# A state-space filter and a gated low-rank feed-forward on one core: first group in a fixed order, two weight sums by transfers, token halves as heads

## The chip, the core and the metric

The kernel runs on one NeuronCore of a Trainium2 chip. The metric is the device time of one execution in microseconds (us). Before the change it is 1004.41 us, the median of three runs (1003.79 to 1004.69).

The core has TensorE (PE: matrix products from SBUF into PSUM), VectorE (DVE), ScalarE (ACT), GpSimd (POOL) and SyncE (SP, which here only issues transfers). ACT and POOL issue transfers as well. All transfers move over 16 DMA engines.

## What is computed

Each of 64 channels h is filtered along 1024 positions with a kernel that comes from 64 complex exponentials, is masked by length, and the 1024-vector of each of 64 x 64 tokens then goes through a gated mixture of 64 low-rank experts:

```python
def cond(u, length, log_dt, C, log_A_real, A_imag, D):     # u: 64 x 64 x 1024
    mask = (jnp.arange(Lq) < length[:, None]).astype(u.dtype)
    u_m = u * mask[:, None, :]
    # K[h, l] = 2 Re sum_n Cs[h, n] exp(dtA[h, n] * l)
    kernel = _get_kernel(log_dt, C, log_A_real, A_imag, Lq)
    y = irfft(rfft(u_m, 2 * Lq) * rfft(kernel, 2 * Lq))[..., :Lq]
    y = y + u_m * D[:, None]
    return y * mask[:, None, :]

def ffn(x, A, B, Wr):                                       # 64 experts of rank 16
    scores = xf @ Wr.T
    top_vals, top_idx = jax.lax.top_k(scores, 16)
    G = zeros(N, 64); G[top_idx] = softmax(top_vals)
    h = jnp.einsum('nd,krd->nkr', xf, A)
    return jnp.einsum('nkr,kdr->nd', h * G[:, :, None], B) * 2.0

out = x + ffn(cond(x, ...), A, B, Wr)
```

A and B are seen as 1024 x 1024 matrices (64 experts times rank 16). All arithmetic is in float32.

## The kernel before

**Groups.** The 64 channels are cut into eight groups of eight (`HG`), so a group has 8 x 64 = 512 tokens (`TOK`). The kernel has two stages: for each group the filter, the gates and the product with A; then, over all groups, the product with B. The change lies in the first stage, and nearly all of it in group 0 and in what comes before it.

**Filter of a group** (`tables`, `conv`). A position is block times 128 plus offset. `tables(g)` makes, for four pairs of channels, the powers `w` of the exponentials (ScalarE: exp, sin, square; VectorE: phases), from them `b`, and by two products with the identity (`pb`, L277 and L279) the matrix `bt` that turns a block into a state. A column of `bt` plus D gives `kc`. Its transpose `pk` (L292) goes by a small transfer to `krows` in DRAM, and is read back as `toep`, a Toeplitz matrix for each channel (L295, L297). `turn` holds the step over one block. `tables` is a generator, and its callers advance it step by step.

`conv(g)` takes pairs of channels. `into_states(i)` (L555, L560) makes the state that each block adds, four products per pair, evicted by ScalarE. `recur` (L563 to L573) carries states over the seven blocks on VectorE: 18 small instructions per pair, two pairs interleaved in group 0. `out_of(i)` multiplies x with `toep` (L581) and the states with `w` (L587) into `pc`, and VectorE masks `pc` into `y` (L593).

**Product with A** (`first`, `seven`). It is a Strassen-Winograd product with seven multiplications instead of eight: left factors from the quarters of A, right factors from the quarters of y. A right quarter is half of the features by half of the tokens. Before, a token half is half of the batch: `y` has the shape `[P, NBLK, NS2, HG, HB]`, and each half takes 32 of 64 batch entries of all eight channels. `right_factors` (VectorE, four instructions) makes the sums. `seven` runs the products in the order 1, 6, 2, 7, 5, 4, 3 for each of two row ranges j (0 and 2); each product is eight matmuls. Products 1 and 2 accumulate in one bank, 5 and 3 in another. Product 1 reads right quarter 11, product 2 quarter 21, with the left factors a11 and a12, and neither needs a sum.

**Left factors.** `quarters` (L156) loads the quarters of A on SP's queue, eight transfers of 512 KB, and x tiles follow. `factors_by_identity` (L182) forms s1 = a21 + a22, s2 = a11 + s1 and s4 = a12 + s2 in four PSUM banks, by products with the identity, then a11 + a21 into the place of a21. ScalarE copies each bank out. Product 3 uses s4, and product 7 the new a21.

**Gates** (`gates`, `spread_gates`). Scores `psh` (L640), `psc` (L649), the top 16 by `max` and `match_replace` on VectorE, softmax; a transpose `pg` (L685), a copy, a transfer to `gt_dram`, and eight loads of 256 KB (`gx`, POOL's queue) that spread each gate over 16 rows. `finish` multiplies the products with `gx` on POOL (L719) and, for quarter 11, on VectorE (L726).

**What sets the order.** A scheduler orders the instructions of each engine ahead of time; within an engine they then run in that order. Parts are held as written: `manual_schedule(engines={V.engine})` (`first_order`, L355) fixes VectorE from the parameters to the mask (L475), and `keep_in_program_order` fixes single instructions. PSUM pools limit what may be in flight: `ps_f` has four banks (sums, products, and `pc` of odd pairs of group 0), `ps_c` two (`pc`), `ps_k` two (`pb`, `pk`, `pu`, scores).

The start is written as: parameters together with six steps of `tables(0)` (L419), the scales alpha and beta (L458), all s1, s2 and s4 sums (L463), the rest of `tables(0)` (L466), the mask (L469 to L473). Then `conv(0)` runs with the remaining sums as its steps, then `gates(0)`, `first(0)`.

Of the kernel before, what the change touches and what calls it, by code (L numbers as in the profile page):

```python
# [44 lines left out]
P = 128  # L45
# [14 lines left out]
HB = NB // NS2  # L60
# [32 lines left out]
def body(ctx: ExitStack, tc, x, xo, lens, par, dvec, at, bm, wt, cst, out):  # L93
# [62 lines left out]
    def quarters(wpool, w, name, queue):  # L156


        where = (("s3", 1, 0), ("a22", 1, 1), ("a11", 0, 0), ("a12", 0, 1))
        a = [factor(wpool, name, t) for t, m, k in where]  # L160

        def load(n, i):
            t, m, k = where[n]
            tc.keep_in_program_order(queue.dma_start(
                a[n][:, i : i + 2, :],
                w[:, k * KH + i : k * KH + i + 2, m * (L // 2) : (m + 1) * (L // 2)],
            ))

        for n, i in ((0, 0), (1, 0), (0, 2), (1, 2), (2, 0), (2, 2), (3, 0), (3, 2)):
            load(n, i)  # L170
        return a
# [10 lines left out]
    def factors_by_identity(a21, a22, a11, a12, out):  # L182
# [14 lines left out]
        for k in range(KH):  # L197
            add(banks[k], a11[:, k, :])
            nc.scalar.copy(s2[:, k, :], banks[k])
            yield  # L200
        for k in range(KH):
            add(banks[k], a12[:, k, :], last=True)
            nc.scalar.copy(s4[:, k, :], banks[k])
            yield
        for k in range(KH):
            bank = ps_c.tile([P, L // 2], F32, tag="pc", name=f"sum3_{k}")
            add(bank, a11[:, k, :], first=True)
            add(bank, a21[:, k, :], last=True)
            nc.scalar.copy(a21[:, k, :], bank)
            yield  # L210
# [4 lines left out]
    wa_quarters = quarters(wp, at, "wa", nc.sync)  # L215
# [9 lines left out]
    def tables(g):  # L225
# [37 lines left out]
        bt = tp.tile([P, GP, 2 * P + 2], F32, tag="bt", name=f"bt_{g}")  # L263
        kc = tabp.tile([P, HG], F32, tag="kc", name=f"kc_{g}")
        for i in range(GP):
# [5 lines left out]
            nc.scalar.activation(b[:, 0, :], re, AF.Copy, scale=alpha[:, j : j + 1])  # L271
            nc.scalar.activation(b[:, 1, :], re, AF.Copy, scale=nbeta[:, j : j + 1])
# [8 lines left out]
            nc.scalar.copy(bt[:, i, :], pb)  # L281
            yield
        turn = tab2.tile([P, 3, GP], F32, tag="turn", name=f"turn_{g}")
        V.tensor_copy(turn[:, 0:2], w[:, :, :, P])
        ts(turn[:, 2], turn[:, 1], -1.0, ALU.mult)
        h0 = g * HG
        tt(kc.rearrange("p (i a) -> p i a", a=2), bt[:, :, 2 * P :],
           d_sb[:, h0 : h0 + HG].rearrange("p (i a) -> p i a", a=2), ALU.add)
        yield
        row = krows[h0 : h0 + 1, :]  # L290
        pk = ps_k.tile([HG, P], F32, tag="pk", name=f"pk_{g}")
        nc.tensor.matmul(pk, lhsT=kc, rhs=ident, start=True, stop=True)  # L292
        ks = tabp.tile([HG, P], F32, tag="ks", name=f"ks_{g}")
        nc.scalar.copy(ks, pk)
        nc.sync.dma_start(krows[h0 : h0 + HG, P - 1 :], ks)  # L295
        toep = tp.tile([P, HG, P], F32, tag="toep", name=f"toep_{g}")
        nc.sync.dma_start(  # L297
            toep, bass.AP(row.tensor, row.offset, [[1, P], [KROW, HG], [1, P]]))
# [57 lines left out]
    first_order.enter_context(tc.manual_schedule(engines={V.engine}))  # L356
    log_both = par_sb[:, 0:2, :].rearrange("p a h -> p (a h)")
# [59 lines left out]

    steps0 = tables(0)
    together(some(steps0, 6), real_part(), angle())  # L419
# [41 lines left out]
    wa, wb = [], []  # L461
    marks = {}
    sums = factors_by_identity(*wa_quarters, wa)  # L463
    for _ in some(sums, 12):
        pass
    for _ in steps0:  # L466
        pass

    lens_f = prep.tile([P, NB], F32, tag="lensf", name="lens_f")  # L469
    V.tensor_copy(lens_f, lens_sb)  # L470
    mask = const.tile([P, NBLK, NB], F32, tag="mask", name="mask")
    tt(mask, feat.unsqueeze(2).to_broadcast([P, NBLK, NB]),
       lens_f.unsqueeze(1).to_broadcast([P, NBLK, NB]), ALU.is_lt)  # L473
# [681 lines left out]
```

## Time and profile before

| | |
|---|---|
| median of three runs | 1004.41 us |
| the profiled execution, whole | 1004.42 us |
| its span | 1002.6 us, 12158 instructions |
| granted TensorE clock | 0.998 |
| span up to psh of group 0 | 55.87 us |
| TensorE busy from 0 to 30, 30 to 56 us | 23.21 and 24.62 us |
| VectorE busy in the same | 18.55 and 22.64 us |
| TensorE busy from 56 to 135 us | 78.78 of 79 us |
| transfers before x6 has landed | 6.8 MB by 22 us |

The span is that of the instructions; the time of the execution has 1.8 us around it. A line of the time line gives start, length from the first to the last of its instructions, engine, source line, operation, tiles out<-in with their shapes, and the number of instructions; square brackets hold the idle time before it and what ended it. One fp32 matmul is two instructions. A line of the stages gives the window, its length, the busy time and number of instructions of PE, PEld, DVE, ACT and POOL, then granted clock, busy share of the 16 DMA engines and GB/s. Names in this profile are those of the program without their numbers: `was`, `waa` are quarters and sums of A, `h` a product with A, `s` a state (before 560 us), `ty` a right factor, `p_...` a parameter.

### The profile page before, as it was taken

To read this page: it belongs to the slowest core of one execution; us is meant where nothing else is said; L and a number is where in the kernel's file an instruction comes from. 1 tells how busy PE (TensorE), PEld (TensorE's weight loads), DVE (VectorE), ACT (ScalarE), POOL (GpSimd) and SP (SyncE) were. 2 spreads that over 40 slices of the span, in tenths; PEclk is the share of its full clock that TensorE was granted. 3 is DMA by queue.
4 is the path that set the end of the run, shared out by engine and by line. 5 is a ranking of instruction groups with operands and counts; after the bars stand their busy time and mean duration, and the time that the engine had idled before them with its cause. 6 is when DMAs were issued, how large, how long until landed. Compare 5 with 4: busy or idle time off the path is not lost.

```text
span 1002.6 us, 12158 instructions
## 1 busy us (share of the span) xinstructions
PE 985.1 (98%) x4416; PEld 738.4 (74%) x4416; DVE 717.5 (72%) x1672; ACT 165.8 (17%) x339; POOL 330.8 (33%) x278
## 2 busy tenths in 40 slices
PE   7999999999999999999999999998999999999998
PEld 3367666686676676677677578887888888888887
DVE  6887778587587587676646649778965786686674
ACT  5436041131141041031001100000000000000000
POOL 0002023122123113114103202245655673654555
PEclk9999999999999999999999999999999999999999
DMA  7113316315405315315315154473474367267432
GB/s 273 64 53 112 126 42 184 137 52 154 137 22 184 118 40 163 137 43 163 115 65 158 48 198 163 158 272 137 158 264 167 126 211 271 85 210 253 132 119 105
DMA packets 66189, 140.86 MB, mean 140 GB/s; under 512 B 9362, under 2 KB 17874, under 8 KB 66130
## 3 DMA queue, kind: packets, MB, share of 16 engines
q1 hardware_dynamic: 49376, 94.54, 27.4%
q0 software_dynamic: 15744, 44.07, 14.0%
q10 hardware_dynamic: 1010, 1.48, 0.6%
q8 instruction: 35, 0.57, 0.2%
q14 instruction: 24, 0.20, 0.1%
HBM read 92.79 MB, written 47.25 MB: 140 GB/s over the span
## 4 chain that ended last, share of the span: by engine, by line
PE 96%; DVE 3%; DMA 1%; issue 0%; SPq 0%; DVEq 0%
PE h L502 38%; PE s L933 33%; PE pc L581 6%; PE pc L587 5%; PE pu L555 5%; PE psh L640 3%; PE sum L190 2%; PE pb L277 1%; DMA waa<-in_at 1%; PE psc L649 1%; PE pb L279 1%; DVE t L788 0%; DVE y L593 0%; PE pg L685 0%; PE pk L292 0%
## 5 line engine op out<-in xcount | busy, mean ns | idle before, releaser
L318 DVE SCALAR_TENSOR_TENSOR s<-s,turn 128x64 f32<-128x64 f32 (+1 forms) x576 | 146.0, 303 | 36.7 <-ACT s L560 30.2
L502 PE MATMUL h<-y,waa 128*128 128x256 f32 x512 | 122.7, 384 | 0.0
L502 PE MATMUL h<-y,was 128*128 128x256 f32 x512 | 117.8, 381 | 0.0
L502 PE MATMUL h<-ty,was 128*128 128x256 f32 x512 | 116.4, 380 | 0.0
L502 PEld LDWEIGHTS h<-y,waa 128*128 128x128 f32 x512 | 93.7, 190 | 27.0 <-issue 15.4
L502 PEld LDWEIGHTS h<-y,was 128*128 128x128 f32 x512 | 96.1, 190 | 19.9 <-issue 7.5
L502 PEld LDWEIGHTS h<-ty,was 128*128 128x128 f32 x512 | 96.6, 190 | 16.7 <-issue 3.9
L719 POOL TENSOR_TENSOR hg<-h_p,gx 128x512 f32<-128x512 f32 x16 | 26.8, 1678 | 223.1 <-DVE h_p L318 215.4
L719 POOL TENSOR_TENSOR hg<-h_u,gx 128x512 f32<-128x512 f32 x32 | 49.5, 1546 | 136.2 <-DVE h_u L307 136.1
L593 DVE TENSOR_TENSOR y<-pc,mask 128x512 f32<-128x512 f32 x64 | 42.5, 684 | 37.0 <-PE pc L587 37.0
L947 ACT COPY p<-s 128x512 f32<-128x512 f32 x28 | 16.4, 586 | 317.4 <-PE s L933 317.4
L696 POOL DMA_DIRECT2D gx<-gt_dram x56 | 33.5, 625 | 97.2 <-DMA gt_dram<-gt 90.3
L812 POOL TENSOR_TENSOR o<-o,acc_a 128x512 f32<-128x512 f32 x32 | 48.5, 1535 | 47.8 <-ACT acc_a L830 21.7
L581 PE MATMUL pc<-x,toep 128*128 128x512 f32 x128 | 62.0, 607 | 0.0
L502 PE MATMUL h<-ty,waa 128*128 128x256 f32 x256 | 58.8, 382 | 0.0
L307 DVE TENSOR_TENSOR hg<-hg 128x512 f32<-128x512 f32 x64 | 42.8, 689 | 21.4 <-POOL hg L719 20.5
L560 ACT COPY s<-pu 128x448 f32<-128x448 f32 x64 | 33.9, 532 | 140.8 <-PE pu L555 140.4
L587 PE MATMUL pc<-s,w 64*128 64x448 f32 x256 | 56.8, 562 | 0.0
L502 PEld LDWEIGHTS h<-ty,waa 128*128 128x128 f32 x256 | 47.9, 190 | 10.7 <-issue 4.6
L555 PE MATMUL pu<-x,bt 128*64 128x448 f32 x256 | 55.5, 553 | 0.0
L812 POOL TENSOR_TENSOR o<-o,b_room 128x512 f32<-128x512 f32 x32 | 49.9, 1580 | 9.8 <-DVE b_room L307 9.8
L307 DVE TENSOR_TENSOR o<-o,s 128x512 f32<-128x512 f32 x52 | 35.4, 681 | 23.6 <-PE s L933 18.5
(225 smaller groups left out, 1627.8 us busy)
## 6 DMA issues: line engine op xcount, KB each, us to landing
x<-in_x SPq DMA_DIRECT2D x32, 512.0 KB
hg_dram<-hg POOLq DMA_DIRECT2D x16, 1024.0 KB, 6.0
o<-in_xo SPq DMA_DIRECT2D x64, 256.0 KB
out<-o SPq DMA_DIRECT2D x64, 256.0 KB
gx<-gt_dram POOLq DMA_DIRECT2D x56, 256.0 KB, 6.6
qy<-hg_dram SPq DMA_DIRECT2D x28, 512.0 KB
r<-hg_dram SPq DMA_DIRECT2D x26, 512.0 KB
hg_dram<-hg POOLq DMA_DIRECT2D x16, 768.0 KB, 4.4
```

The source lines that it names most:

```text
L307: V.tensor_tensor(out=o, in0=a, in1=b, op=o_)
L318: V.scalar_tensor_tensor(out=o, in0=a, scalar=s, in1=b, op0=o1, op1=o2)
L502: nc.tensor.matmul(bank[:, ii, :], lhsT=fac[n - 1][:, k, (j + ii) * P : (j + ii + 1) * P], rhs=rf[n - 1][:, k, :], start=(first and ii == ...
L555: nc.tensor.matmul(pu[hh * NS : (hh + 1) * NS, :], lhsT=bt[:, i, (1 - c) * P + hh * NS : (1 - c) * P + (hh + 1) * NS], rhs=xt[:, hh, : NCH ...
L560: nc.scalar.copy(s[:, c], pu.rearrange("p (k b) -> p k b", b=NB))
L581: nc.tensor.matmul(pc, lhsT=toep[:, 2 * i + hh, :], rhs=xt[:, hh, :], start=True, stop=False)
L587: nc.tensor.matmul(pcs[hh][:, NB:], lhsT=w[o : o + NS, c, i, 1:], rhs=s[o : o + NS, c].rearrange("p k b -> p (k b)"), start=False, stop=(c ...
L593: marks["y"] = V.tensor_tensor(out=y[:, :, :, 2 * i + hh, :], in0=pcs[hh].rearrange("p (k s b) -> p k s b", s=NS2, b=HB), in1=mask.rearran ...
L696: i = queue.dma_start(gx[:, ii, :], gt_dram[g, c * n : (c + 1) * n, :].unsqueeze(1).to_broadcast([n, RANK, TOK]),)
L719: G.tensor_tensor(out=o, in0=a, in1=b, op=op)
L812: tc.keep_in_program_order(G.tensor_tensor(out=o, in0=a, in1=b, op=op_))
L933: nc.tensor.matmul(bank[:, ii, :], lhsT=left_[i - 1][:, k, ii * P : (ii + 1) * P], rhs=right_[i - 1][:, k, :], start=(first and ii == 0 an ...
```

## The change

- **Loads.** The first 1 MB of A comes in four transfers of 256 KB instead of two of 512 KB (`fine`).
- **Sums.** `factors_by_identity` makes s1 and s2 only. `other_sums` adds a11 onto a21 by accumulating transfers from DRAM, loads a12 into the place of s4, and accumulates s2 onto it, six transfers of 512 KB on POOL's queue.
- **Tables of group 0.** `b` is scaled by VectorE instead of ScalarE. `kc`, `pk`, `krows` and `toep` are made for pairs 0 and 1 as soon as their `bt` is there, then for pairs 2 and 3.
- **Order.** ScalarE is held in written order too (`first_copies`), until the sums are done: one sum ahead of the parameters' sine, seven after the scales. `conv(0)` advances `tables(0)` itself, and closes VectorE's written order after the mask.
- **Token halves.** A half is now four of eight channels with all batch entries: `y` is `[P, NBLK, NS2, HH, NB]`, and the host arranges xo and out accordingly. Half 0 is thus complete once pairs 0 and 1 are.
- **Products in group 0.** `out_of` is cut into `inside` (Toeplitz part) and `across` (states). In `seven` product 2 comes second for j = 0 of group 0, and the right factors of that group are made only after it. Product 1 is issued between `inside` and `across` of pairs 2 and 3, product 2 after the `across`. A fourth state tile uses room of `y`.
- **Group 1.** Its tables are issued after the last state copy of group 0 as well as after its last mask.

```diff
-HB = NB // NS2
+HH = HG // NS2
...
+        if fine:
+            for i in range(2):
+                load(0, i, 1)
+                load(1, i, 1)
+        for n, i in ((0, 0), (1, 0), (0, 2), (1, 2), (2, 0), (2, 2), (3, 0), (3, 2))[2 * fine :]:
             load(n, i)
...
         for k in range(KH):
-            add(banks[k], a11[:, k, :])
+            add(banks[k], a11[:, k, :], last=True)
             nc.scalar.copy(s2[:, k, :], banks[k])
             yield
-        for k in range(KH):
-            add(banks[k], a12[:, k, :], last=True)
-            nc.scalar.copy(s4[:, k, :], banks[k])
-            yield
-        for k in range(KH):
-            bank = ps_c.tile([P, L // 2], F32, tag="pc", name=f"sum3_{k}")
-            add(bank, a11[:, k, :], first=True)
-            add(bank, a21[:, k, :], last=True)
-            nc.scalar.copy(a21[:, k, :], bank)
-            yield
+    def other_sums(a21, a22, a11, a12, s4, s2):
+
+        for k in range(0, KH, 2):
+            G.dma_start(a21[:, k : k + 2, :], at[:, k : k + 2, : L // 2], accum_op=ALU.add)
+        for k in range(0, KH, 2):
+            tc.keep_in_program_order(
+                G.dma_start(s4[:, k : k + 2, :], at[:, KH + k : KH + k + 2, : L // 2]))
+        for k in range(0, KH, 2):
+            G.dma_start(s4[:, k : k + 2, :], s2[:, k : k + 2, :], accum_op=ALU.add)
...
+        def rows(i, n):
+
+            w_, row = 2 * (n - i), krows[h0 + 2 * i : h0 + 2 * i + 1, :]
+            pk = ps_k.tile([w_, P], F32, tag="pk", name=f"pk_{g}_{i}")
+            nc.tensor.matmul(pk, lhsT=kc[:, 2 * i : 2 * n], rhs=ident, start=True, stop=True)
+            ks = tabp.tile([HG, P], F32, tag="ks", name=f"ks_{g}_{i}")[:w_, :]
+            nc.scalar.copy(ks, pk)
+            nc.sync.dma_start(krows[h0 + 2 * i : h0 + 2 * n, P - 1 :], ks)
+            nc.sync.dma_start(toep[:, 2 * i : 2 * n, :],
+                              bass.AP(row.tensor, row.offset, [[1, P], [KROW, w_], [1, P]]))
...
-            nc.scalar.activation(b[:, 0, :], re, AF.Copy, scale=alpha[:, j : j + 1])
-            nc.scalar.activation(b[:, 1, :], re, AF.Copy, scale=nbeta[:, j : j + 1])
+            for c, by in enumerate((alpha, nbeta)):
+                if g == 0:
+                    ts(b[:, c, :], re, by[:, j : j + 1], ALU.mult)
+                else:
+                    nc.scalar.activation(b[:, c, :], re, AF.Copy, scale=by[:, j : j + 1])
...
+            if g == 0 and i == 2:
+                kernels(0, 2)
+                rows(0, 2)
             yield
...
+    first_copies = ExitStack()
+    first_copies.enter_context(tc.manual_schedule(engines={nc.scalar.engine}))
...
     steps0 = tables(0)
-    together(some(steps0, 6), real_part(), angle())
+    next(steps0)
+    for _ in some(sums, 1):
+        pass
+    together(some(steps0, 5), real_part(), angle())
...
-    for _ in some(sums, 12):
+    for _ in some(sums, 7):
         pass
-    for _ in steps0:
-        pass
+    first_copies.close()
+    other_sums(*wa_quarters, *wa[2:6:3])
...
         yield
+        if second_early:
+            product(2, c11)
+            yield
         p6 = product(6)
...
+        if g == 0:
+            step(1)
         into_states(0)
         into_states(1)
         if g == 0:
-            step(KH)
+            step(3)
+            masks()
+            first_order.close()
+            step(1)
+            prep_ctx.close()
         recur(0, 1)
         if g == 0:
             into_states(2)
-            out_of(0)
             into_states(3)
+            first_two = inside(0), inside(1)
+            across(*first_two[0], True)
+            across(*first_two[1])
             recur(2, 3)
-            out_of(1)
-            out_of(2)
-            out_of(3)
+            last_two = inside(2), inside(3)
+            yield
+            across(*last_two[0], True)
+            across(*last_two[1])
             return
...
-    for _ in conv(0, sums, got):
+    steps = conv(0, steps0, got)
+    next(steps)
+    hp = pool(left, "hp", 1, "left")
+    y = got.pop()
+    spread = {}
+    products, done = counted(first(0, y, spread)), [0]
+    ahead(products, 1)
+    for _ in steps:
         pass
-    y = got.pop()
-    products = None
+    ahead(products, 1)
...
-                with tc.issue_after(marks["y"].ins):
+                with tc.issue_after(marks["y"].ins), tc.issue_after(marks["s"].ins):
```

## The prediction

> **What bounds the kernel.** The page first: which engine is full, and which engine the last chain runs through.
>
> ```profile
> PE 985.1 (98%) x4416; PEld 738.4 (74%) x4416; DVE 717.5 (72%) x1672; ACT 165.8 (17%) x339; POOL 330.8 (33%) x278
> PE 96%; DVE 3%; DMA 1%; issue 0%; SPq 0%; DVEq 0%
> ```
>
> TensorE is the bound: work taken off it pays, unless it then waits. The waits of TensorE say where it does (total, times, longest):
>
> ```profile
> PE sum L190 <- DMA was<-in_at: 5.5, 1, 5.5
> PE s L933 <- DVE acc_a L307: 3.2, 1, 3.2
> PE psh L640 <- DVE y L593: 1.7, 2, 1.4
> PE pg L685 <- DVE sa L307: 1.3, 1, 1.3
> ```
>
> Almost nothing after the start. The change works in the first 56 us, so I read the time line there (start, length):
>
> ```profile
> 5.54 2.05 PE L190 MATMUL sum<-was,cst_sb 128*128 128x512 f32 x2 [5.54 <-DMA was<-in_at]
> 16.03 8.75 PE L190 MATMUL sum<-waa,cst_sb 128*128 128x512 f32 x20
> 29.75 3.33 PE L555 MATMUL pu<-x,bt 128*64 128x448 f32 x16
> 55.87 3.65 PE L640 MATMUL psh<-y,wt_sb 128*64 128x512 f32 x16 [1.38 <-DVE y L593]
> 63.91 3.62 PE L502 MATMUL h<-ty,was 128*128 128x256 f32 x16
> ...
> 15.94 0.19 DVE L307 TENSOR_TENSOR p_s<-p_s 128x32 f32<-128x32 f32 x1 [1.84 <-ACT p_s L404]
> 24.39 0.35 DVE L318 SCALAR_TENSOR_TENSOR b<-w,p_nbeta,b 128x128 f32<-128x128 f32 x1 [3.34 <-ACT b L271]
> 32.09 10.71 DVE L318 SCALAR_TENSOR_TENSOR s<-s,turn 128x128 f32<-128x128 f32 x44 [1.74 <-ACT s L560]
> ```
>
> Before psh at 55.87 TensorE is never idle after 8.8, yet VectorE waits on ScalarE at 14 to 24 us, because ScalarE is evicting sums. Two chains run side by side: TensorE's work, and parameters, b, states, recurrence, masks on VectorE. Removing TensorE work leaves the second, so both have to be timed.
>
> **TensorE's account.** One weight-sum matmul (two instructions) costs 0.86 us warm (8.77 us for ten from 16.03). The sums s4 (4) and a21 (8) go: 12 x 0.86 = 10.3 us. Two products move ahead of psh; one is 3.46 us (16 instructions, 0.216 us apart), so 6.9 us is done early. One more small pk costs 0.3 us. Work before psh was 55.87 - 5.54 - 1.22 - 1.38 = 47.7 us; it becomes 44.6, of which 6.9 later work. If TensorE idled as before (8.1 us), the gain would be about 10 us. The question is the idle time.
>
> **VectorE's chain, dated step by step** from the instruction order of the changed program and the durations above:
> - The fixed ScalarE order puts one eviction, not two, ahead of the sine table. The two waits on ScalarE (1.84 and 0.24 us) go: the scales end at 20.95 - 2.1 = 18.9.
> - b of group 0 moves to VectorE: per pair two tensor_scalar at about 0.14 (between the 0.09 that a 32-wide one holds the engine and the 0.34 of a 516-wide one) and two scalar_tensor_tensor at 0.29, so 0.86. Four end at 22.3; a first pair at 19.8 feeds TensorE, where before the first was at 24.8. The 3.34 us wait goes. VectorE pays 8 x 0.14 = 1.1 us, in time it spent waiting. Kernel column, turn and mask (0.6) bring it to 23.6.
> - pu of pairs 0 and 1: 1.65 us each from 21.1, ScalarE 0.53 behind each bank: the second state is ready at 25.1. The recurrence proper starts there, not at 32.09.
> - Each half of the recurrence is 36 instructions at 0.243 (10.71/44), 8.75 us; with the few that start alone, the first ends at 33.0. In the meantime TensorE does pb, pk, pu of pairs 2 and 3 and four toep products (1.91 a pair) until 33.9, then across pairs 0 and 1 (1.71 each) until 37.3.
> - The second half, with four masks (0.60 apart) between: 33.0 to 44.2. TensorE waits for the first masks (ps_c has two banks) from 37.3 to 38.9, runs toep of pairs 2 and 3 to 42.7, waits 0.3 for y of pair 1, then product 1 (43.0 to 46.5), across (49.9), product 2 (53.3). The last mask ends at 51.3, so psh no longer waits: 53.3 instead of 55.87, **2.55 us earlier with 6.9 us of products done: 9.5 us**.
>
> **Toeplitz in two halves.** The trace has one transfer of 512 KB, issued at 31.46 and moving until 34.7, 3.2 us. The half has its kernel rows by 25.7, is issued near 27.1 and lands by about 29.6; TensorE asks at 30.1. SP has nothing else queued there: the x loads of the next group come behind, and wait for TensorE anyway. The cover is 0.5 us; each us beyond is paid.
>
> **Transfers in place of sums.** No row shows an accumulating transfer. The a21 sum and the s4 load and sum are 3.1 MB on POOL's queue, issued from about 10 us, once the s1 products have read a21. Product 7 wants them near 61, so their own time is hidden, and POOL has nothing until the gate loads at 72. What they can hurt is the x loads:
>
> ```profile
> 18.00:19.00 1.00, 1.00 (x3) 0.38 (x2) 0.76 (x4) 1.00 (x3) 0.00 (x0) 1.00 1.04 394
> 22.00:23.00 1.00, 1.00 (x4) 0.47 (x3) 0.00 (x0) 1.00 (x4) 0.00 (x0) 1.00 0.00 0
> ```
>
> The DMA share is 1.04 until 20 us: the engines are full while these transfers come in. Adding up the rows, x of pairs 0 and 1 lands at about 16.4 and 18; they are needed at 21.1 and 22.75. The Trainium skill, "DMA: Bandwidth & Descriptors", section "Issuing engines are not separate DMA queues", says that transfers of all issuers share the same engines and interleave. By it, at half of 390 GB/s, x arrives at 21.6 and 24.3: 1.5 us is paid. If the cover by the row alone held, 0. The ends are 0 and 2.7 (everything shared from 10 us on). I take **1.5**, since the row shows no free engine.
>
> **Clock.** The first sums at 5.54 took 1.19 us an instruction, later ones 0.59: the array starts cold, at half speed. The trace has one later gap of a like size, in the product with B, and the stages behind it (first figure behind the busy times: granted clock) show what it costs:
>
> ```profile
> 681.46 3.46 PE L933 MATMUL s<-b_room,ey 128*128 128x256 f32 x8 [3.23 <-DVE acc_a L307]
> ...
> 681.00:682.00 1.00, 0.55 (x2) 0.52 (x3) 1.00 (x3) 0.00 (x0) 0.00 (x0) 0.91 1.07 436
> 682.00:683.00 1.00, 1.00 (x3) 0.73 (x3) 1.00 (x3) 0.00 (x0) 0.00 (x0) 0.50 0.55 221
> ```
>
> 3.23 us of idleness, then half speed for some 3.4 us (681.9 to 685.3): 1.7 us lost. The Trainium skill, "TensorE: Matmul & The Clock Gate", Part 1, puts the bound at about 3.4 us of idleness, in windows that run freely. Both speak against this change: TensorE now idles at about 13.5 to 15.3 and 18.2 to 19.8, with 3 us of work between. By row and rule each gap is too short, 0; if a window with so little work counts as idle, pb and pu from 19.8 run at half speed for 3.4 us and the states come 1.7 us later. I take 0.
>
> **After psh.** The gates need psc, then 7.6 us of VectorE (61.46 to 69.04); TensorE has 22 matmuls of products against 20 before, 9.5 us. VectorE has w and b for the next group between, so pg waits about **0.5 us**. VectorE then meets the gating of c11, a wait for the gate load, ahead of kc, on which pk and all of TensorE behind it hang. The first two gate loads land 3.9 us after issue:
>
> ```profile
> gx<-gt_dram POOLq DMA_DIRECT2D x2, 256.0 KB, 3.9
> ```
>
> Issued at about 72, they are there at 76.3; TensorE reaches pk at 78. Hidden by 1 us. In group 1 TensorE has 21 matmuls between pu of pair 1 and pu of pair 2, as before; from group 2 on its order is the old one. The layout leaves mask, products and transfers their sizes, and the mask writes runs of 64 instead of 32. I cost that at 0: VectorE has room in the groups (52 of 75 us busy from 210 to 285), so a change of either sign in its 0.68 is covered by TensorE.
>
> **Sum.** 9.5 - 1.5 - 0.5 = 7.5 us. The profiled execution took 1004.42 with a span of 1002.6, so 1.8 us lies outside; it is the median (1004.41). Span 995.1, time **996.9 us**.
>
> **Rivals.**
> - *A slower start.* States arrive later still, by the cold array (1.7) and the later x of pair 1 (2.7 instead of 1.5); VectorE's chain hands it on whole. For it: full DMA engines, two new gaps. Against: the gaps are short. Gain 7.5 - 2.9 = 4.6: about 999.8.
> - *Given back in group 0 and 1.* The products that used to cover gates and gate loads are spent: if pg, kc and the group 1 recurrence each wait about 2.2 us (between the 1.3 of pg and the 3.2 of the longest late wait above), 6.6 go: about 1003.5. Against: 21 or 22 matmuls still lie there.
> - *Slower: accumulation starves x.* If an accumulating byte holds a DMA engine long enough, x of pair 1 is late by more than the gain. Gain ends when it lands 9 us after 22.75, at 32. From 10 us on 22 us x 390 GB/s = 8.6 MB of engine time; the loads up to that x need 3.0, leaving 5.6 for 1.05 plain and 2.1 accumulated: it decides from 2.2 times a plain byte, if served ahead of x. At 3 times (7.4 + 3.0 MB, 26.6 us from 10) x lands at 36.6, 13.9 late in all against 1.5 counted: 996.9 + 12.4 = about 1009. For it: no row prices accumulation. Against: queues interleave, and half of the accumulation waits for s2 and the s4 load.
>
> **How the numbers follow.** Forecast 63%, slow start 19%, given back 10%, starved 8%. A measurement of this kernel tells 0.2%, 2 us, from no change. The first two are faster; of the third a part lies on each side of 1002.4: faster 0.87, same 0.06, slower 0.07. The range goes from 993.8 (no contention, no pg wait, and 1 us of VectorE's chain over-counted) to 1001.8 (the slow start, and one of the waits of the next rival with it).
>
> **What would show it.** Right: no psh wait, psh near 53 to 55 with two h products before it; 24 fewer sum instructions; the first long recurrence at 25 to 27; TensorE idle before psh 8 to 12 us. x late: pu waits for in_x. Cold: pb or pu at twice 0.39 and 0.54 us an instruction. Given back: waits of pg or pk on VectorE over 2 us. The forecast is wrong if psh comes after 58, or if groups beyond 1 change length.

## The result, and the profile after

The changed kernel took 1002.38 us (median of 12 executions, 996.38 to 1005.30), beside 1004.18 us for the kernel before, measured with it. The ratio is 0.997, with a 95% interval from 0.9956 to 0.9983: faster by a little, and far from the 996.9 us of the forecast. Four more executions of the same kernel (e11 below) gave 998.68 us, so the median of all 16 is 1000.8. The two intervals for this one kernel (the other is 0.9927 to 0.9956) only touch, so that a difference of two or three us between medians proves little here without its profile. The kernel before spreads over 2 us, this one over 9. The profiled execution took 1004.54 us, with a span of 1002.8: it lies near the upper end of the range, and its loss is larger than that of the median.

The page of the changed kernel: busy time by engine, and the engines of the chain that ended last.

```profile
PE 977.8 (98%) x4394; PEld 736.2 (73%) x4394; DVE 716.7 (71%) x1681; ACT 160.1 (16%) x324; POOL 334.4 (33%) x284
PE 91%; DMA 4%; DVE 3%; issue 0%; POOL 0%; ACT 0%; SPq 0%; DVEq 0%
```

TensorE has 22 instructions and 7.3 us less to do, as the diff says (24 of sums go, two of pk come). But transfers now hold 4% of the chain instead of 1%. The waits of TensorE (total, times, longest) name them:

```profile
PE pu L601 <- DMA x<-in_x: 4.0, 2, 3.8
PE pu L601 <- ACT s L606: 2.9, 2, 2.2
PE pk L287 <- DVE kc L338: 2.4, 3, 1.5
PE pc L627 <- DMA toep<-krows: 1.5, 1, 1.5
PE psh L702 <- DVE y L644: 0.3, 1, 0.3
PE pg L747 <- DVE sa L338: 0.3, 1, 0.3
```

The waits for y and sa that the change was to shorten are nearly gone (1.7 to 0.3 us, 1.3 to 0.3). In their place stand x (4.0), toep (1.5) and two that come through ScalarE and VectorE (2.9, 2.4). The time line dates them (start, length, instructions, idle time before and what ended it):

```profile
19.79 0.49 PE L309 MATMUL pb<-cst_sb,b 128*128 128x130 f32 x2
...
21.70 1.72 PE L601 MATMUL pu<-x,bt 128*64 128x448 f32 x8 [0.24 <-DMA x<-in_x]
27.19 3.25 PE L601 MATMUL pu<-x,bt 128*64 128x448 f32 x8 [3.77 <-DMA x<-in_x]
30.37 0.80 PE L309 MATMUL pb<-cst_sb,b 128*128 128x130 f32 x2
...
39.83 3.70 PE L627 MATMUL pc<-x,toep 128*128 128x512 f32 x8 [1.54 <-DMA toep<-krows]
...
60.61 3.65 PE L702 MATMUL psh<-y,wt_sb 128*64 128x512 f32 x16
```

The first tables come at 19.79, as forecast (19.8). Then x of pair 1 is 3.8 us late, the same eight instructions take 3.25 us instead of 1.72, toep is late too, and psh starts at 60.61 instead of the forecast 53.3 (54.8 with the late x that was priced in). The windows of 1 us (busy time of PE, PEld, DVE, ACT, POOL, then granted clock, DMA share, GB/s) show what happened to the transfers and the clock:

```profile
22.00:23.00 1.00, 1.00 (x8) 0.35 (x4) 1.00 (x6) 0.30 (x1) 0.00 (x0) 1.00 1.10 257
26.00:27.00 1.00, 0.00 (x0) 0.00 (x0) 0.00 (x0) 0.00 (x0) 0.00 (x0) 0.50 1.05 418
32.00:33.00 1.00, 1.00 (x5) 0.88 (x4) 0.25 (x1) 0.27 (x2) 0.00 (x0) 0.59 0.95 172
```

At 22 us, where the DMA engines stood idle before, they are full and move only 257 GB/s. At 26 us no compute engine does anything, and TensorE's clock has been cut to 0.50; the 0.59 of the last row puts its return at 32.8.

### The profile page after: what moved, and what is told of

Same layout as the page of the kernel before. It is cut to its first block, busy times and chain, and to the rows that moved or that the text cites. A ratio compares the mean times of both kernels' runs of the same rounds, so it can differ in the third digit from the quotient of the medians.

```text
span 1002.8 us, 12115 instructions
## 1 busy us (share of the span) xinstructions
PE 977.8 (98%) x4394; PEld 736.2 (73%) x4394; DVE 716.7 (71%) x1681; ACT 160.1 (16%) x324; POOL 334.4 (33%) x284
## 4 chain that ended last, share of the span: by engine, by line
PE 91%; DMA 4%; DVE 3%; issue 0%; POOL 0%; ACT 0%; SPq 0%; DVEq 0%
PE h L536 37%; PE s L1002 33%; PE pc L627 6%; PE pc L636 5%; PE pu L601 5%; PE psh L702 3%; DMA x<-in_x 2%; DMA was<-in_at 1%; PE psc L711 1%; PE pb L309 1%; PE pb L311 1%; DMA gx<-gt_dram 0%; DVE t L857 0%; PE pg L747 0%; DMA toep<-krows 0%; DMA krows<-ks 0%
## 5 line engine op out<-in xcount | busy, mean ns | idle before, releaser
L349 DVE SCALAR_TENSOR_TENSOR s<-s,turn 128x128 f32<-128x128 f32 (+1 forms) x558 | 143.8, 306 | 40.4 <-ACT s L606 34.4
L785 POOL TENSOR_TENSOR hg<-h_u,gx 128x512 f32<-128x512 f32 x32 | 47.2, 1475 | 117.1 <-DVE h_u L338 117.0
L636 PE MATMUL pc<-s,w 64*128 64x448 f32 x248 | 54.7, 561 | 0.0
L606 ACT COPY s<-pu 128x448 f32<-128x448 f32 x62 | 32.8, 532 | 129.9 <-PE pu L601 129.6
```

The lines of the kernel that those rows point to most:

```text
L349: V.scalar_tensor_tensor(out=o, in0=a, scalar=s, in1=b, op0=o1, op1=o2)
L606: marks["s"] = nc.scalar.copy(s[:, c], pu.rearrange("p (k b) -> p k b", b=NB))
L636: m = nc.tensor.matmul(pcs[hh][:, NB:], lhsT=w[o : o + NS, c, i, 1:], rhs=s[o : o + NS, c].rearrange("p k b -> p (k b)"), start=False, sto ...
L785: G.tensor_tensor(out=o, in0=a, in1=b, op=op)
```

## The experiments

The theory (A): the new order earns what was forecast, and the six transfers take it back by delaying x, lens, krows and toep; an accumulating transfer holds the DMA engines longer than a plain one of the same size, and the clock is halved behind the wait that it makes. The main rival (B): the order itself is worth less than computed. "psh" in the table is the start of group 0's psh in the profiled execution, "to group 1" the time from there to group 1's.

| kernel | median us (lowest to highest, runs) | ratio to before, 95% interval | psh | to group 1 |
|---|---|---|---|---|
| changed | 1002.38 (996.38 to 1005.30, 12) | 0.9970 (0.9956 to 0.9983) | 60.61 | 78.53 |
| e11, the same | 998.68 (997.10 to 1001.81, 4) | 0.9942 (0.9927 to 0.9956) | 58.48 | 76.85 |
| e1 late | 995.24 (992.36 to 999.51, 6) | 0.9918 (0.9898 to 0.9938) | 52.52 | 76.84 |
| e2 none | 993.75 (993.45 to 994.09, 4) | 0.9898 (0.9885 to 0.9910) | 52.64 | 75.98 |
| e3 plain | 997.45 (995.22 to 998.73, 5) | 0.9931 (0.9919 to 0.9943) | 55.80 | 76.71 |
| e4 x first | 1000.86 (998.11 to 1002.79, 6) | 0.9967 (0.9954 to 0.9979) | 58.40 | 77.93 |
| e5 behind x | 994.00 (992.16 to 997.80, 6) | 0.9901 (0.9886 to 0.9916) | 52.41 | 75.99 |
| e6 split | 996.77 (994.54 to 1000.19, 6) | 0.9929 (0.9914 to 0.9944) | 54.88 | 77.61 |
| e7 x, lens first | 1000.57 (997.56 to 1002.37, 6) | 0.9960 (0.9947 to 0.9974) | 61.03 | 75.99 |
| e8 sums only | 1003.96 (1003.21 to 1006.07, 13) | 1.0005 (0.9997 to 1.0013) | 55.55 | 78.11 |
| e9 order only | 1004.71 (1002.42 to 1008.56, 13) | 1.0012 (1.0000 to 1.0024) | 61.51 | 75.98 |
| e10 warm | 1003.35 (999.53 to 1005.25, 21) | 0.9990 (0.9981 to 0.9998) | 58.44 | 76.78 |
| e12 e5 gated | 995.81 (995.20 to 999.57, 6) | 0.9924 (0.9909 to 0.9938) | 52.62 | 76.18 |
| e13 changed, gated | 1001.09 (997.08 to 1002.95, 8) | 0.9966 (0.9953 to 0.9979) | 59.97 | 76.12 |
| e14 warm, half | 1000.89 (997.68 to 1003.50, 7) | 0.9963 (0.9949 to 0.9977) | 57.14 | 78.49 |

### Does the order earn it? (e2, e1)

e2 leaves the six transfers out:

```diff
-            G.dma_start(a21[:, k : k + 2, :], at[:, k : k + 2, : L // 2], accum_op=ALU.add)
+            pass
```

and so with the others; product 7 then reads a21 without a11, and product 3 reads a12 in place of s4.

> The six transfers left out: product 7 uses a21 without a11 added, product 3 uses a12 in place of s4. Theory A: the same as holding them back, within 1 us, so 994.5 to 997; the difference of this run and the one before it is what the transfers cost where nothing waits for them. Rival B: above 1000, and spread as before.

993.75 us, all four runs within 0.7 us. The time line of e2:

```profile
21.49 3.33 PE L600 MATMUL pu<-x,bt 128*64 128x448 f32 x16
...
31.72 3.70 PE L626 MATMUL pc<-x,toep 128*128 128x512 f32 x8
...
52.64 3.65 PE L701 MATMUL psh<-y,wt_sb 128*64 128x512 f32 x16
```

Both pairs of pu run in one piece, toep is there when it is asked, and psh starts 8.0 us earlier than in the profiled changed kernel. The order is worth the forecast (993.75 is even a little under what was expected of e2); rival B falls. e1 keeps the transfers, but holds their issue back until the second half of toep has landed:

```diff
-    other_sums(*wa_quarters, *wa[2:6:3])
...
+            gate = G.tensor_copy(..., toep[:, HG - 1, :1])
+            with tc.issue_after(gate.ins):
+                other_sums(*wa_quarters, *wa[2:6:3])
```

> The same program, with the six transfers of the weight sums held back on POOL until the second half of the Toeplitz matrices of group 0 has landed. Theory A (these transfers share the DMA engines with x, krows and toep and delay all three): x of pair 1 lands before 22.9 us, no wait of pu for in_x over 0.3 us, krows lands within 1.5 us of its issue, psh of group 0 at 52.5 to 54.5, time 994.5 to 997, and runs that agree within 2 us. Rival B (the long gaps and the half clock come from the new instruction order itself, whatever the transfers do): granted clock still at 0.50 between 20 and 33 us, time above 1000.

995.24 us, psh at 52.52: the work of the transfers is the same, only its place is not, and the start is whole again. The runs, expected within 2 us, spread over 7.

### Bytes, or the addition? (e3)

The same six transfers without the addition; the sums are not made, a21 is overwritten.

```diff
-            G.dma_start(a21[:, k : k + 2, :], at[:, k : k + 2, : L // 2], accum_op=ALU.add)
+            G.dma_start(a21[:, k : k + 2, :], at[:, k : k + 2, : L // 2])
```

> The same six transfers at the same places and sizes, without the addition (a21 is overwritten by a11, s4 ends as s2). Theory A1 (bytes alone: 3.1 MB more on full engines): x of pair 1 lands at 25 to 27, time within 1 us of the changed kernel, 1001 to 1003. Theory A2 (the addition makes a byte dearer): the DMA rate stays at about 390 GB/s through 17 to 24 us instead of 255, x of pair 1 lands 1.5 to 3 us earlier, time 997 to 1000.

997.45 us. By the medians bytes alone cost 3.7 us over e2, the addition 4.9 more by the first 12 runs of the changed kernel (3.3 by all 16). The stage that was read above, in e3 (columns as there):

```profile
22.00:23.00 1.00, 0.79 (x5) 0.41 (x7) 1.00 (x6) 0.00 (x0) 0.00 (x0) 1.00 1.02 378
```

The engines are about as full, but move 378 GB/s instead of 257. How much longer an accumulated byte holds them can be read by queue. The changed kernel from 16 to 22 us (queue, packets, MB, share of the time of 16 engines; q0 is POOL's, here with the a21 accumulation, q1 is SP's, with x):

```profile
q0 software_dynamic: 365, 0.71, 64.1%
q1 hardware_dynamic: 594, 0.90, 46.2%
```

One MB took the 16 engines 5.4 us on q0 and 3.1 on q1. On q0 of e3, without the addition, it took 2.6 (1.40 MB at 61.6% in the same window). An estimate from these: one accumulated byte is worth 1.8 to 2.1 plain ones.

The addition shows less in x than was expected: x of pair 1 came at 26.24 in e3, only 0.2 to 1.0 us earlier than in the two profiles of the changed kernel. But psh came 2.7 to 4.8 us earlier, since e3 had no half clock (1.00 throughout; TensorE's gap before that x was 2.3 us) and no wait for toep.

### Can x simply go first? (e4, e7)

e4 queues x of pairs 0 and 1 ahead of the last weight quarter; e7 x of all pairs and lens:

```diff
+            if fine and (n, i) == (3, 0):
+                load_x(0)
+                tc.keep_in_program_order(nc.sync.dma_start(lens_sb, lens.partition_broadcast(P)))
+                load_x(2)
...
```

> x of pairs 0 and 1 queued on SP ahead of the two a12 loads, the six transfers where they were. Theory A: both x tiles land by about 20, pu waits less than 1 us, the clock stays at 1.00 up to 26 us; what is left is the delay of krows and toep behind the accumulation (about 2.5 us of the present loss), time 996.5 to 999.5. Rival B: above 1001.

> As e4_x_first, but x of all four pairs and lens stand ahead of the two a12 loads. Theory A (lens behind a12 was what ate e4's gain): no wait for x and none of kc for lens; the accumulations start later, behind a12, and meet krows and toep, whose landing costs 1 to 3 us: 995.5 to 998.5, psh at 54 to 56 us. Rival E (the additions slow whatever load comes last, so that any order only moves the loss): 1000 to 1002 again, with the wait at toep (4 us or more) and a half clock around 36 to 40 us.

Neither helped (1000.86 and 1000.57; 996.5 to 999.5 had been expected of e4). In e4 no wait for x is left, but the small lens load behind it was late, and with it the masks, kc and pk. The time line of e4:

```profile
26.58 0.20 DVE L512 CAST lens_f<-lens_sb 128x64 f32<-128x64 int32 x1 [3.23 <-DMA lens_sb<-in_lens]
...
30.36 0.59 PE L290 MATMUL pk<-cst_sb,kc 128*4 128x128 f32 x2 [3.82 <-DVE kc L341]
```

Behind that wait the clock is 0.50 again, from 30.4 to 37.2.

In e7 x and lens were on time, and it was the Toeplitz tables' turn:

```profile
37.77 6.18 PE L631 MATMUL pc<-x,toep 128*128 128x512 f32 x8 [3.00 <-DMA toep<-krows]
```

6.18 us instead of 3.70 is the half clock again. Here it began at 32.6, before this wait: the longest gap from 20 us until then was 1.95 us (TensorE waiting for the krows write through ScalarE's `ks`), with 1.0 us of work between it and a gap of 0.6. I had expected 995.5 to 998.5 from e7; the other reading of its expectation, that any order only moves the loss, was right for the orders tried: with the additions among the first loads, some load that was due came last each time.

### Where may they run? (e6, e5)

e6 starts a21's accumulation when x of the fourth pair has landed and s4's after toep; e5 starts all six when the last x tile of group 1 has landed, near 45 us.

```diff
+            for h in range(HG, 2 * HG, 2):
+                load_x(h)
+            gate = G.tensor_copy(..., x_tiles[2 * HG - 2][:, 1, :1])
+            with tc.issue_after(gate.ins):
+                other_sums(*wa_quarters, *wa[2:6:3])
```

> The two accumulating transfers of a21 wait for x of the fourth pair (about 22 us) and so run in the quiet stretch after the x tiles; the four of s4 wait for the second half of toep (about 31 us). Theory A: x and lens are on time, what may be late is krows and toep if a21's accumulation (4 to 8 us) still runs at 26 to 30 us: 994 to 997, with a wait of pc for toep of 0 to 2 us. Rival D (the transfers hurt only because they stand in front of x): 993.5 to 994.5, no wait for toep. A value of 999 or more would say that the stretch of 22 to 28 us is as sensitive as that before it.

> All six transfers of the weight sums are held back until the last x tile of group 1 has landed (some 45 us); the first sum is asked at about 60 us, the second at about 74 us, and one such transfer landed 4.6 to 14.2 us after its issue in the runs so far. Theory A (what is lost is what the transfers take from x, lens, krows and toep at the start): nothing of the start is touched, neither are group 1's x tiles, so the time is that of the kernel without the six transfers, 993.5 to 995, psh at about 52.6 us, and the spread of 7 us that e1_late still had shrinks to some 2. Rival C (the transfers cost by themselves wherever they run, through slower matmuls or a late sum): 997 or more, with a wait of psh or pg for a21 or s4. Should the transfers land after 60 us, psh or pg would show a wait on a DMA of a21 or s4 and the time rises by just that.

e6 took 996.77, at the upper end of its range. Ahead of psh it lost 2.4 us, to krows and toep alone (a wait of 1.0 us for the krows write, through `ks`, and of 1.3 for toep): these loads are sensitive too. The rest lies behind psh (77.61 in the last column). e5 took 994.00, like e2 without the transfers: what they cost is their place. No wait for a21 or s4 appears. This version beats both kernels, the one before by 1.0%, the changed one by 0.7% (its 16 runs) or 0.8% (its first 12). Its spread, which I expected to shrink to 2 us, stayed at 5.6.

### Each half alone (e8, e9)

e8 is the kernel before with the six transfers instead of the twelve sums, e9 the changed kernel with all sums on TensorE and no transfers for them.

> The kernel before with one part of the change alone: the twelve sums of TensorE are left out and the same six transfers stand in their place; the order of the first group, the tables and the two moved products are as before. Theory A: TensorE is rid of 12 times 0.86 us, 10.3 us, of which the transfers give back about what they gave back in the changed kernel (8.6 us) or less: 994 to 1003, likeliest 1000, with a wait for x of pair 1 of 2 us or more. Rival B2 (in the old order the first loads stand elsewhere and the transfers hide): 994 to 996 and no wait for x above 1 us. Rival F (the sums ran in time in which TensorE had to wait anyway, so that their removal alone gains nothing): 1004 or more, and it is the new order that earns the 10.5 us of e2_none.

> The other half alone: the order of the first group, the tables a pair at a time and the two early products as in the changed kernel, but all weight sums stay on TensorE (four single ones ahead of the first table, four double ones between the second pair's output and the third's), and there are no transfers for them. Theory A (neither half earns by itself: the sums' removal gained nothing in e8_sums_only since TensorE then waited for the tables, and the order gains nothing while TensorE still has to make the sums): e2_none's 993.75 plus 12 times 0.86 us, less the 1 to 2 us of waits that they can fill, 1002 to 1004. Rival G (the order alone earns most of the gain, and the sums' transfers are superfluous): 994 to 998, with the sums found in time in which TensorE would have waited.

Neither earns anything: 1003.96 and 1004.71. In e8 TensorE is rid of the sums and waits for the old chain of VectorE instead:

```profile
23.17 0.80 PE L277 MATMUL pb<-cst_sb,b 128*128 128x130 f32 x2 [2.85 <-DVE b L318]
...
55.55 3.65 PE L641 MATMUL psh<-y,wt_sb 128*64 128x512 f32 x16 [1.37 <-DVE y L594]
```

10.3 us of work removed move psh by 0.3. There was no wait for x at all: the old order asks for it too late for that. But e8 is not clean. 2.2 us into this wait TensorE's clock falls to 0.50, and it comes back at 32.7:

```profile
24.00:26.00 2.00, 2.00 (x10) 1.84 (x9) 0.63 (x3) 1.38 (x5) 0.00 (x0) 0.50 1.09 276
30.00:32.00 2.00, 2.00 (x8) 0.50 (x6) 0.00 (x0) 0.53 (x1) 1.59 (x2) 0.50 0.37 70
```

Its pb and its first pu run at half speed, and the recurrence starts at 32.75, where the kernel before had 32.09. What e8 would earn at full clock was not tested. In e9 the chain is fast and TensorE is full again:

```profile
13.85 8.75 PE L194 MATMUL sum<-waa,cst_sb 128*128 128x512 f32 x20
...
61.51 3.65 PE L714 MATMUL psh<-y,wt_sb 128*64 128x512 f32 x16
```

psh comes 8.9 us later than in e2, with the same two products done. As measured, the gain of 10 us belongs to both halves together, which is what two chains of nearly the same length would show; for e9 the profile shows it plainly, for e8 the half clock has a part that is not separated. I had put e8 at 1000 as the likeliest.

### The price of the half clock (e10, e14), and a second look (e11)

Extra matmuls that nothing reads fill TensorE's wait for x of pair 1: six in e10, three in e14.

```diff
         into_states(0)
+        if g == 0:
+            spare = ps_f.tile([P, L // 2], F32, tag="pf", name="spare")
+            for _ in range(3):
+                tc.keep_in_program_order(nc.tensor.matmul(
+                    spare, lhsT=ident, rhs=wa[0][:, 0, :], start=True, stop=True, skip_group_check=True))
         into_states(1)
```

> The changed kernel with six more matmuls of TensorE (6 times 0.43 us, 2.6 us, into a bank that nothing reads) between the states of pair 0 and pair 1, that is in the wait for x of pair 1 that the changed kernel's trace shows at 23.4 to 27.2 us. They shorten nothing but TensorE's idle stretch, from 3.8 to some 1.2 us. Theory A (the wait also halves the clock for 6 us, which costs 2 to 3 us): 999 to 1000.5, and a granted clock of 1.00 from 20 to 40 us. Rival H (the half clock lies beside work that waits for VectorE or transfers anyway and costs nothing): 1002 to 1003. Where x comes early, the six matmuls themselves cost up to 2.6 us, so the fastest runs should be slower than 996.4.

> The changed kernel unaltered, for a second profile: its times spread over 9 us and the first profile was of a run near the top. Theory A (the spread is that of the landing of x of pair 1, krows and toep, and of the half clock that follows): the difference of the two profiled runs is found ahead of psh, as a different wait for x, kc or toep and a different stretch at half clock, and from psh on they agree within 0.5 us but for the clock after the late gap near 680 us. Rival I (the spread comes from the later groups): psh starts at the same time in both.

> e10_warm with half its extra matmuls: each of them is two records of 0.43 us, so that the six of e10_warm filled 5.4 us and ran past the landing of x by up to 2 us; three fill 2.6 us of the wait of 3.3 to 3.8 us. Theory A (the wait's half clock costs some 2 us ahead of psh): granted clock 1.00 from 20 to 40 us, psh at 56.5 to 58 us instead of 58.5 to 60.6, and 999.5 to 1001.5. Rival H (the half clock costs nothing that is not waited for anyway): psh at 58.5 or later and 1002 to 1003.5.

e10 overshot: one such matmul is two instructions, so that six took 5.4 us, past the landing of x. Its 1003.35 is therefore no measure of what the half clock costs. e14 fits the gap. Its time line:

```profile
23.02 2.84 PE L661 MATMUL spare<-waa,cst_sb 128*128 128x512 f32 x6
26.35 1.72 PE L601 MATMUL pu<-x,bt 128*64 128x448 f32 x8 [0.49 <-DMA x<-in_x]
```

and the same place in e11, the second profile of the unaltered kernel:

```profile
26.48 3.08 PE L601 MATMUL pu<-x,bt 128*64 128x448 f32 x8 [3.31 <-DMA x<-in_x]
...
58.48 3.65 PE L702 MATMUL psh<-y,wt_sb 128*64 128x512 f32 x16
```

x came at the same time in both (26.35 and 26.48). With the array kept busy pu takes 1.72 us and psh starts at 57.14; with the idle gap 3.08 and 58.48. Of the 1.34 us of difference 0.13 is the landing, so 1.2 us is the net gain, after part of it is lost again at toep, for which e14 waits 1.31 us and e11 0.88. From the start of this pu to psh, less that wait, the three profiles whose clock stayed at 1.00 (e3, e10, e14) take 29.5 to 29.6 us, e11 with 3.4 us at half clock 31.1, and the first profile with 6.8 us of it 31.9. The half clock thus costs some 1.6 us in the one and 2.3 in the other. The granted clock in e14 is 1.00 from 20 to 40 us. By its times (1000.89, beside 1000.8 for all 16 runs of the changed kernel) e14 shows no gain; it rests on the profile, and its next interval happened to be a long one (78.49).

### A second source of the spread (e12, e13)

e11 was to show that the two profiles of the changed kernel agree from psh on. They do not: from group 0's psh to group 1's it is 78.53 us in the first and 76.85 in the second. The table's last column has values from 75.98 to 78.53 in kernels that share the new order. From group 1's psh to the last group's, all these profiles agree to 0.03 us in every group. The time line of the changed kernel in group 1's tables:

```profile
86.53 2.16 DVE L349 SCALAR_TENSOR_TENSOR f<-cst_sb,p_tulo,f 128x129 f32<-128x129 f32 x4
88.72 1.37 DVE L345 TENSOR_SCALAR f<-f 128x516 f32<-128x516 f32 x1
...
87.11 1.42 POOL L785 TENSOR_TENSOR hg<-h_p,gx 128x512 f32<-128x512 f32 x1 [3.38 <-DMA gx<-gt_dram]
```

and of e2:

```profile
77.83 1.14 DVE L348 SCALAR_TENSOR_TENSOR f<-cst_sb,p_tulo,f 128x129 f32<-128x129 f32 x4
79.00 0.43 DVE L344 TENSOR_SCALAR f<-f 128x516 f32<-128x516 f32 x1
...
79.39 1.26 POOL L784 TENSOR_TENSOR hg<-h_p,gx 128x512 f32<-128x512 f32 x1 [3.52 <-DMA gx<-gt_dram]
```

Where gx lands early, GpSimd's gate product runs beside VectorE's operations on f, and these take 3.53 us together instead of 1.57. ScalarE's sine waits for f, the states wait behind the sine, TensorE for the states: the longest of the "ACT s" waits above, 2.2 us. e12 (on e5) and e13 (on the changed kernel) make GpSimd wait for the last operation on f:

```diff
+                with tc.issue_after(marks["f1"].ins):
+                    gt_(b22, c22, gate(1, 1), ALU.mult)
```

> e5_behind_x1 with one more wait: GpSimd's first product with the gates in group 0 begins after VectorE's last operation on f of the tables of group 1. In four profiles GpSimd began it between 0.6 us after f's first operation and just after its last, and where it began early VectorE's operations on f took 540 and 1370 ns instead of 285 and 430 ns and group 1's first psh came up to 2.5 us later (78.53 us after that of group 0 in the changed kernel, 75.98 in e2_none, 76.84 in e1_late). Theory J (this coincidence is most of the spread that e1_late and e5_behind_x1 still had): 992 to 993.5, highest run at most 2.5 us above the lowest, psh of group 1 75.9 to 76.1 us after that of group 0. Rival K (the spread is that of the half clock near 680 us or of something not seen): the median stays at 994 and the spread at 5 us or more.

> The changed kernel with the same one wait and nothing else. Theory J: its psh of group 1 comes 76 us after that of group 0 instead of 76.85 and 78.53 in the two profiles, so the median falls by 1 to 2 us, to 1000 to 1001.5, while the loss ahead of group 0's psh (58 to 61 us instead of 52.6) stays. Rival K: 1002 to 1003, unchanged.

The interval became 76.18 and 76.12 us. e12 is no test, since e5 had 75.99 without the wait; e13 is one, against 78.53 and 76.85. Its time line:

```profile
85.43 1.15 DVE L350 SCALAR_TENSOR_TENSOR f<-cst_sb,p_tulo,f 128x129 f32<-128x129 f32 x4
86.61 0.43 DVE L252 TENSOR_SCALAR f<-f 128x516 f32<-128x516 f32 x1
86.85 1.33 POOL L786 TENSOR_TENSOR hg<-h_p,gx 128x512 f32<-128x512 f32 x1 [3.77 <-DVE f L350]
```

The other profiles bear it out. In all six of the new order in which these operations on f took 1.57 or 1.58 us (e2, e5, e7, e9, e12, e13) the interval is 75.98 to 76.18; in the eight in which GpSimd began earlier and they took longer it is 76.71 to 78.53. So the cause of this part is shown. That it explains the spread is not: e12's median, 995.81, missed its range and is no better than e5's; five of its runs lie within 2.1 us, the sixth at 999.57 with a mean clock of 0.995. e13's 1001.09 had been expected, but is not apart from the 1000.8 of all runs unaltered. The clock is a candidate for what else moves single executions. In e5's profile it is at 0.50 near 670 us for 6.8 us, in e2's for 3.4, and from the last psh to the end e5 takes 1.2 us longer; of e5's six runs the three fastest have a mean clock of 1.000, the slowest 0.996. No run tests it. In two runs of e12 time outside the span (2.9 and 3.1 us instead of 1.8) is a part.

## Why the prediction was wrong

The direction was right, the size was not: the forecast gain was 7.5 us; 1.8 came by the first comparison, 3.4 by the median of all 16 runs. 1002.38 lies above the stated range, 1000.8 within it, near an upper end of 1001.8 (the slow start of 999.8 and a wait of 2.2 add up to 1002.0). The prediction's own sign of being wrong, psh after 58, came in both profiles: 60.61 and 58.48.

**TensorE's account and VectorE's chain: right.** 9.5 us less 0.5 for pg were forecast for the order without contention; e2 gives 10.2 (its ratio of 0.9898 on 1004). psh comes at 52.64 where 53.3 was written, pg waits 0.3 instead of 0.5.

**"Transfers in place of sums: I take 1.5": the step that failed.** It stood for all that the transfers delay, with ends at 0 and 2.7. By the medians they cost 8.6 us (first 12 runs) or 7.0 (all 16), some five times as much. Three things were wrong in it:
- *Size of the delay.* The forecast had x of pair 1 land at 24.3, by halving a rate of 390 GB/s. It came at 27.19 and 26.48. Until 16 us POOL's queue moved nothing: of the 2.77 MB from 9 to 16 us 2.76 are on q1. From 17 to 24 us it took about half of the packets (483 of 981) and 0.96 of 1.79 MB. So SP's queue, with x, was left 119 GB/s, not 195: the bytes were nearly halved, but of a rate of 256. In e3 it had 147. The Trainium skill's sentence in "DMA: Bandwidth & Descriptors", section "Issuing engines are not separate DMA queues", that transfers of all issuers share the engines, agrees; the halving of a rate that stays at 390 was my own addition.
- *Price of a byte.* It was left at that of a plain one in the forecast and given to the third rival, which turned from 2.2 times on. The estimate above is 1.8 to 2.1. That rival's mechanism was the one that happened; at 1009 it had too much of the accumulation running ahead of x. The s4 additions waited for s2 and ran from 28.5 us on, as the text argued against the rival.
- *Only x was priced.* lens, krows and toep share the engines too. The first krows write, 2 KB, was followed by the issue of toep, which waits for it, after 3.6 us instead of 1.2 (32.44 to 36.02, in e2 26.16 to 27.36).

In the first profile the loss against e2 closes. Ahead of psh it is 8.0 us: pu of pair 1 starts 4.1 us later (27.19 for about 23.1), the half clock behind it costs 2.3, toep 1.5. Up to group 1's psh 2.5 more come from GpSimd beside VectorE. Together that is the 10.5 us between the spans of 1002.8 and 992.3. In e11 the four are 3.4, 1.6, 0.9 and 0.9, of 7.1 between the spans.

**Toeplitz in two halves: cover of 0.5 us.** In e2 toep is on time, as computed. With the transfers TensorE waited 1.54 us (0.9 in e11). The text said that each us beyond the cover is paid, but put nothing on the engines that carry it.

**Clock: 0 taken.** pb does run at full speed at 19.79, but this was not put to the test: the gaps forecast for 13.5 to 19.8 us did not come. TensorE is busy throughout from 13 to 20 us in the changed kernel, because its sums run later than forecast (the last twelve instructions from 14.49 to 19.80). The lateness of x makes a gap of its own, of 3.3 to 3.8 us, which the forecast didn't connect with the clock. It is at 0.50 afterwards, as in the row at 681 us behind 3.23 us of idleness, and this costs 1.6 and 2.3 us. The Trainium skill's bound of about 3.4 us in "TensorE: Matmul & The Clock Gate", Part 1, fits these gaps only roughly, and others not: in e8 the clock fell in a gap of 2.85 us, in e7 behind one of 1.95 with little work before it, while in e3 a gap of 3.09 us near 675 left it at 1.00. The case that the forecast named and set aside, that a window with little work counts as idle, fits e7. (The slow first sums, which the forecast calls a cold array, stand in rows with a granted clock of 1.00 in the kernel before; these rows don't show why they are slow.)

**Group 1.** "Hidden by 1 us" was said of the gate load ahead of kc; pk indeed waits little (0.18). That the same load landing early slows VectorE's tables was not seen: 2.5 us in one profile.

**The rivals.** The slower start (999.8) is nearest to the median of all runs. Both of its terms came, a later x and a cold array, but larger than it had them (4.1 us for 2.7, 2.3 for 1.7, in the first profile), through the starvation's mechanism, and with the cold stretch behind x and not at 19.8. Beside them stood toep and group 1, which it did not have. That its sum is near is in part luck.

## What to carry to other kernels

In this kernel, work moved from TensorE to a transfer was free only where the transfer could be late and no other load was due (e5). Before such a move, count all bytes issued before a load that is due, take the addition at its measured price, and check every small load in the stretch, not the largest alone. Then hold the transfer back behind the last load that is due, as e5 does, rather than put that load first. Where two chains run side by side at nearly the same length, shortening either alone can show nothing (e9, and e8 with its half clock), so neither half should be judged by itself.

## What was not expected of the hardware

- With the a21 accumulation among the loads, the DMA engines are full (share 1.10 to 1.12) at 251 to 262 GB/s, where plain transfers move 373 to 408 (e3); adding from SBUF to SBUF at 31 us it is 197 GB/s at a share of 1.04.
- The clock fell to 0.50 at 26.0 us in the first profile, 2.6 us into the gap; in e11 at 26.7, when work had just begun again. It stayed there for 3.4 us in e11, 6.8 in the first profile and 10.2 in e7 and e8.
- Four VectorE operations of 285 ns took 540 each, and one of 430 ns 1370, while GpSimd products of 128x512 ran beside them.
